# A point-cloud attention kernel: gathers put first in GpSimd's iteration, second-layer maxima subtracted by VectorE, and an inverse root by Newton steps

## The chip, the cores and the metric

The kernel runs on one core of a Trainium2 chip. The metric is the device time of one execution in microseconds (us), the median of several runs. The engines are named as in the profile: PE (TensorE matmuls) and PEld (its weight loads), DVE (VectorE), ACT (ScalarE), POOL (GpSimd) and SP (SyncE, which here only issues DMAs).

## The reference

The reference is a chain of six blocks on `x` of shape (2, 64, 1024). Each reads a layer norm of `x` and adds its result to `x`: a quantised cross attention, a Mamba block, an expert layer, the point-cloud network (`L1_xattn`), a block-masked linear layer and a gated feed-forward layer. The change lies in the point-cloud network. There are two batches of N = 1024 points with 64 features each. Four orderings of the points (two Morton curves and two Hilbert curves) give each point four lists of k = 10 neighbours. Cut to what matters:

```python
def _get_graph_features(feats, inds_list, perm, W_lin, b_lin, k=K):
    for inds in inds_list:                     # four orderings
        neigh = gather(feats, inds)            # B, N, k, C
        gf = concatenate([broadcast(center), neigh - center], axis=-1)
    x = stack(per_method)[..., perm].reshape(B * N, k, total)
    qh = x.astype(float16).astype(float32).reshape(B * N, k, nheads, 64)
    scores = einsum('bihd,bjhd->bhij', qh, qh) / sqrt(64)
    attn = softmax(scores, axis=-1)
    out = einsum('bhij,bjhd->bihd', attn, qh)
    return (out @ W_lin.T + b_lin).reshape(B, N, k, 128)

g1 = _get_graph_features(f0, inds_list, perm1, W_lin1, b_lin1)
h1 = lrelu(instance_norm(einsum('oc,bnkc->bonk', W_conv1, g1)))
feats1 = h1.max(axis=-1)                       # the same again for layer 2, with
...                                            # 128 channels, and a last product
```

The instance norm takes mean and variance over all points and neighbours of a batch, so a batch's first layer has to be finished before its second begins.

## The kernel before

`mamba` (to about 503 us in the trace) holds the first three blocks, `point_cloud` (503 to about 1080 us) the network above, `masked_linear_and_ffn` the rest. The order of every engine's instructions is the order in which the Python code issues them: a manual schedule, with an in-order queue for each engine, and semaphores where one engine needs what another wrote.

`point_cloud` runs four phases: layer 1 for batch 0 and batch 1 (phases 0 and 1), then layer 2 for the same (2 and 3). A phase is 22 sets of 48 points (the last has 16), so there are 88 items, and `iteration(i)` is a software pipeline over them. In one iteration:

- `edges(i + 2)`: POOL subtracts centres from neighbours (`x`, L964); `mended` corrects the first points of a phase on DVE (L974, L976).
- `apart(i + 1)`: the halves of `x` are copied into block form `xz`, the upper half first (layer 2: DVE, L985; layer 1: ACT, L987), the lower half by ACT (L987).
- `turn(i - 2)`: DVE transposes the attention (`at`, L1018). `collect(i - 4)`: DVE takes statistics (L1083) and maxima over neighbours (L1085) of the finished output in PSUM; where a phase ends, `finish` follows.
- `exponentials(i - 1)`: PE adds minus the row maxima to the scores in PSUM, as a product of a negative identity with the broadcast maxima (L1005); ACT takes the exponential (L1007).
- `scores(i)`: PE writes the mask and the products of the edges with themselves into PSUM (L993, L996). `normalize(i - 1)`: DVE sums and inverts (L1012, L1013), POOL multiplies (L1014). `maxima(i)`: DVE (L1000).
- `attend(i - 3)` (PE L1059, L1062, ACT copy L1064), `weighted(i - 1)` (PE: L1032 in layer 1; L1043 with ACT copies L1045 in layer 2), `turn_u` (DVE L1049, layer 1), `back(i - 3)` (PE L1072).

Work that belongs to the next phase is not in this loop's body but in `plan`, a list of (time, closure) pairs that `neighbours` writes. Times are counted in iterations:

```python
def iteration(i):
    todo(i - 0.5)        # everything in plan with a time up to i - 0.5
    edge(i + 2)
    ...
    todo(i)              # everything up to i
```

`neighbours(ph, perm, start)` plans, for a phase that starts at iteration `start`: the features' transposition and the rows' way through DRAM (`begin`, `begin1`, with eight loads of `cen` on SP's queue, L870, at `start - 14.5`), the centre terms (L888 to L904), and the window of neighbours. For this window each of 8 chunks of 128 points takes four indirect DMAs, issued by POOL (`gather`, L925), then a copy on ACT (`rows`, L932), two transposes on PE (`turn`, L937) and a copy out of PSUM on ACT (`put`, L942). Gather m of chunk c has the time `start - lead + (4c + m) * 2 // 3`, so one or two gathers fall to an iteration.

`finish` turns a phase's statistics into mean and inverse deviation, normalises and applies the leaky ReLU. It returns closures that `plan` spreads over the iterations that follow. `rstd` joins the statistics on DVE (L144), takes a square root on ACT (L146) and the reciprocal on DVE (L148). In layer 1 ACT also brings the two halves of `hm` (64 partitions each) together in one tile (L1132 to L1137). The exponential and the square root need different function tables on ACT.

In the last eight iterations with other work (78 to 85) POOL also masks the weights of the next block (L1365), one 128x1024 product in each, behind L1014.

Of the kernel before, what the change touches and what calls it, by code (L numbers as in the profile page):

```python
# [20 lines left out]
P = 128  # L21
D = 1024
KC = D // P
NB = 2
S = 64
EPS = 1e-5
# [10 lines left out]
NP = 1024  # L37
K = 10
NM = 4
TP = 3  # L40
QP = 4 * TP
SG = 48
NBK = SG // TP
# [49 lines left out]
class Kernel:  # L93
# [47 lines left out]
    def rstd(self, pool, st, p=P):  # L141
        nc = self.nc
        mv = self.t(pool, [P, 2], tag="ln_mv")
        nc.vector.bn_aggr(mv[:p], st)  # L144
        sd = self.t(pool, [P, 1], tag="ln_sd")
        nc.scalar.activation(sd[:p], mv[:p, 1:2], AF.Sqrt, bias=self.eps[:p], scale=1.0)  # L146
        r = self.t(pool, [P, 1], tag="ln_r")
        nc.vector.reciprocal(r[:p], sd[:p])  # L148
        return mv[:, 0:1], r

    def layernorm(self, pool, tag="h", update=None):

# [686 lines left out]
    def neighbours(self, ph, perm, start):  # L839
# [4 lines left out]
        nc, ps, layer, b = self.nc, self.g_ps, ph["layer"], ph["b"]  # L844
        o = 64 * layer
        plan = []
# [73 lines left out]
        def gather(c, m):  # L920
            def work():
                if m == 0:
                    ph[c] = self.t(self.g_feat, [P, NM, 64], tag="sl", bufs=3)
                k = self.place[:, b, perm[m], c:c + 1]
                nc.gpsimd.indirect_dma_start(out=ph[c][:, m, :], out_offset=None, in_=ph["src"][:, :],  # L925
                                             in_offset=bass.IndirectOffsetOnAxis(ap=k, axis=0))
            return work

        def place(c):
            def rows():  # L930
                pm = ph["pm"] = self.t(self.g_feat, [P, 4, NM, 16], tag="pm", bufs=2)
                nc.scalar.copy(pm, ph[c].rearrange("p m (h f) -> p h m f", h=4))  # L932

            def turn():
                pm, pt = ph["pm"], self.t(ps, [P, 2, P], tag="misc")
                for hp in range(2):
                    nc.tensor.transpose(pt[:, hp, :], pm[:, 2 * hp:2 * hp + 2].rearrange("p h m f -> p (h m f)"), self.ident)  # L937
                ph["placed"] = pt

            def put():  # L940
                win = ph["win"].rearrange("p n a -> p a n")
                nc.scalar.copy(win[:, :, LPAD + P * c:LPAD + P * c + P], ph["placed"])  # L942
                if c == KC - 1:
                    e = LPAD + NP
# [12 lines left out]

# [31 lines left out]
    def scores(self, it):  # L989

        nc, x, xz, nb = self.nc, it["x"], it["xz"], it["nb"]
        sc = it["sc"] = self.t(self.g_pa, [P, NBK, 32], tag="sc")[:, 0:nb]
        nc.tensor.matmul(sc, self.ident16, self.mask16.unsqueeze(1).to_broadcast([P, nb, 32]), start=True, stop=False, skip_group_check=True)  # L993
        for k in range(nb):
            for hp in range(2):
                nc.tensor.matmul(sc[64 * hp:64 * hp + 64, k, :], xz[:, hp, k].rearrange("p a j -> p (a j)"), x[:, hp, k, :], start=False, stop=False, skip_group_check=True)  # L996

    def maxima(self, it):
        mx = it["mx"] = self.t(self.g_a, [P, NBK], BF16, tag="mx")[:, 0:it["nb"]]
        self.nc.vector.tensor_reduce(mx, it["sc"], AX.X, ALU.max)  # L1000

    def exponentials(self, it):

        nc, nb = self.nc, it["nb"]
        nc.tensor.matmul(it["sc"], self.nident16, it["mx"].unsqueeze(2).to_broadcast([P, nb, 32]), start=False, stop=True, skip_group_check=True)  # L1005
        e = it["e"] = self.t(self.g_a, [P, NBK, 32], tag="e")[:, 0:nb]
        nc.scalar.activation(e, it["sc"], AF.Exp, scale=0.125)  # L1007

    def normalize(self, it):
        nc, nb, e = self.nc, it["nb"], it["e"]  # L1010
# [92 lines left out]
    def norm_lrelu(self, dst, src, mean, r):  # L1103
        nc = self.nc
        nc.vector.tensor_scalar(dst, src, mean, r, ALU.subtract, ALU.mult)
        nc.vector.scalar_tensor_tensor(dst, dst, 0.2, dst, ALU.mult, ALU.max)

    def finish(self, ph):

        nc = self.nc  # L1110
        hm, st, ns = ph["hm"], ph["st"], len(ph["sets"])
        if ph["layer"] == 2:
            f = hm.rearrange("p g n -> p (g n)")[:, :NP]

            def measure():
                ph["stats"] = self.rstd(self.g_hm, st)

            return [measure] + self.norm_lrelu(f, ph, slice(0, P))
# [6 lines left out]
        left = NP - 2 * QP * ng  # L1125

        def measure():
# [12 lines left out]

    def norm_lrelu(self, f, ph, r):
        nc = self.nc

        def norm():
            mean, rs = ph["stats"]
            nc.vector.tensor_scalar(f, f, mean[r], rs[r], ALU.subtract, ALU.mult)

        def lrelu():
            nc.vector.scalar_tensor_tensor(f, f, 0.2, f, ALU.mult, ALU.max)
            ph["out"] = f  # L1150

        return [norm, lrelu]

    def point_cloud(self):
        nc, tc, a = self.nc, self.tc, self.a
        with ExitStack() as es:
            pool = lambda n, b, **k: (self.ctx if k.get("space") is PSUM else es).enter_context(tc.tile_pool(name=n, bufs=b, **k))
# [21 lines left out]
            mean, r = self.rstd(self.g_hm, self.xst)  # L1179
# [68 lines left out]
            def iteration(i):  # L1248


                todo(i - 0.5)
                edge(i + 2)
                if at(i + 1):
                    self.mended(at(i + 1))
                    self.apart(at(i + 1), 1)
                if at(i - 2):
                    self.turn(at(i - 2))
                if at(i - 4):
                    it = at(i - 4)
                    ph, end = it["ph"], it["last"]  # L1260
                    self.collect(it)
                    if end:
                        work = self.finish(ph)
                        if i == last + 3:
                            for w in work:
                                w()
                        else:
# [240 lines left out]
```

## Time and profile before

| | |
|---|---|
| Median of 3 runs | 1145.97 us (1141.42 to 1148.03) |
| Profiled execution: its own time | 1150.54 us |
| Profiled execution: span, first to last instruction | 1148.5 us |
| Mean granted TensorE clock | 0.96 |
| PE / DVE / ACT / POOL busy in the span | 89% / 67% / 53% / 44% |
| L1005 (the matmul that the change removes in layer 2) | 88 in all, 84 of 128x512, mean 390 ns |
| Function table loads on ACT between 503 and 1062 us | 6, 1283 ns each |
| Gathers L925 | 128, mean 996 ns on POOL |

A line of the timeline gives start, length, engine, source line, operation, tiles written and read, and in brackets how long the engine had been idle before and what ended that. A windows line gives the stretch and its length, then the busy time and the number of instructions of PE, PEld, DVE, ACT and POOL, the granted clock, the DMA share and GB/s. Shapes are partitions x elements.

### The profile page before, as it was taken

Reading aid. Unit: us, or ns where it says so; the run is one execution under the profiler, and the core shown is the slowest. Engines: PE = TensorE matmul, PEld = TensorE weight load, DVE = VectorE, ACT = ScalarE, POOL = GpSimd, SP = SyncE. Lnnn points to the kernel's source line nnn. Section 1 sums busy time; section 2 is a strip of 40 time slices with the busy share of each in tenths; the row PEclk is TensorE's granted clock in tenths of the full one; section 3 lists DMA queues with packets and bytes.
Section 4 is the critical chain, followed back from the end, with each engine's and each line's share of the span. In section 5 each row is a group of like instructions: output and inputs, shape, how many; then the busy total and the mean of one; then the engine's idle time right before and its main releaser. Section 6 shows DMA issues by size and latency. Waiting matters only on the chain.

```text
span 1148.5 us, 34713 instructions
## 1 busy us (share of the span) xinstructions
PE 1019.3 (89%) x15331; PEld 752.1 (65%) x15331; DVE 769.6 (67%) x1623; ACT 611.3 (53%) x977; POOL 510.7 (44%) x421
## 2 busy tenths in 40 slices
PE   3899999999999998966877788878998899999898
PEld 1798958769688695533544545557777777788443
DVE  6698865777767764444867887897666767676511
ACT  6333326576575731125756576657676676776110
POOL 0010110102425175068968788786756577683000
PEclk9999989999999998987988889899999999999999
DMA  8677839687596874723221003100303200000460
GB/s 334 264 273 286 344 135 397 242 351 291 232 403 238 341 297 144 245 48 62 51 32 23 12 11 67 35 16 11 66 7 115 81 13 11 9 4 3 180 260 18
DMA packets 48018, 170.93 MB, mean 149 GB/s; under 512 B 26438, under 2 KB 27378, under 8 KB 40956
## 3 DMA queue, kind: packets, MB, share of 16 engines
q1 hardware_dynamic: 37980, 151.83, 35.6%
q10 hardware_dynamic: 3744, 12.65, 3.2%
q0 software_dynamic: 6144, 4.24, 2.1%
q8 instruction: 120, 1.97, 0.7%
q14 instruction: 30, 0.25, 0.1%
HBM read 163.48 MB, written 2.72 MB: 145 GB/s over the span
## 4 chain that ended last, share of the span: by engine, by line
PE 63%; DVE 15%; issue 7%; ACT 7%; POOL 5%; DMA 3%; DVEq 0%; SPq 0%; ACTq 0%; POOLq 0%
PE pin L346 13%; PE misc L1043 11%; PE po L483 7%; PE op L1062 6%; PE sc L996 3%; PE pt L1072 3%; DVE cpre L361 3%; PE sc L1389 3%; PE misc L1032 2%; POOL sl L925 2%; PE misc L1389 2%; POOL x L964 2%; PE op L1059 2%; DVE df L775 2%; ACT xz L987 2%
## 5 line engine op out<-in xcount | busy, mean ns | idle before, releaser
L346 PE MATMUL pin<-hT,w 128*128 128x128 f32 x2320 | 264.8, 276 | 2.0 <-issue 1.7
L346 PEld LDWEIGHTS pin<-hT,w 128*128 128x128 f32 x2320 | 262.7, 193 | 5.6 <-issue 4.9
L964 POOL TENSOR_TENSOR x<-win,cen 128x960 f16<-128x960 f32 x88 | 170.9, 1942 | 5.0 <-ACT win L942 2.8
L1043 PE MATMUL misc<-wz,xz 128*64 128x128 bf16 x4128 | 131.6, 220 | 17.2 <-issue 10.4
L987 ACT COPY xz<-x 64x1024 f16<-64x1024 f16 (+1 forms) x131 | 133.8, 1021 | 18.3 <-DVE x L974 13.3
L925 POOL DMA_INDIRECT sl<-src,place x128 | 127.5, 996 | 31.5 <-issue 20.3
L1014 POOL TENSOR_TENSOR e<-e,z 128x512 f32<-128x512 f32 x88 | 90.6, 1030 | 112.6 <-DVE z L1013 86.2
L1043 PEld LDWEIGHTS <-xz 128*64 128x64 f16 x4128 | 118.9, 110 | 31.5 <-issue 31.2
L1045 ACT COPY u<-misc 128x512 f32<-128x512 f32 x172 | 98.0, 588 | 52.9 <-PE misc L1043 32.3
L460 POOL TENSOR_TENSOR xc<-y,normw 128x512 f32<-128x512 f32 x8 | 8.3, 1038 | 243.5 <-DVE y L458 200.9
L776 ACT ACTIVATE df<-df,neg 128x1024 f32<-128x1024 f32 x64 | 73.4, 1148 | 76.1 <-DVE df L775 62.5
L483 PE MATMUL po<-ow,xc 128*128 128x512 f32 x240 | 109.4, 609 | 0.0
L1062 PE MATMUL op<-u,at 128*32 128x64 f32 (+1 forms) x2752 | 93.1, 257 | 17.6 <-issue 17.5
L361 DVE SCALAR_TENSOR_TENSOR cpre<-craw,convw,cpre 128x126 f32<-128x126 f32 (+2 forms) x240 | 80.6, 357 | 24.3 <-ACT cpre L355 18.7
L759 POOL DMA_INDIRECT place<-cst,rank x64 | 67.0, 1046 | 51.8 <-DVE rank L781 23.7
L1062 PEld LDWEIGHTS op<-u,at 128*32 128x32 f32 x2752 | 65.1, 113 | 33.3 <-issue 26.0
L1083 DVE BATCH_NORM_STATS2 st<-pt 128x6 f32<-128x240 f32 (+1 forms) x84 | 43.4, 517 | 64.7 <-PE pt L1072 57.5
L775 DVE SCALAR_TENSOR_TENSOR df<-hi_r,hl,lo_r 128x1024 f32<-128x1024 f32 x64 | 80.8, 1291 | 3.3 <-DMA lo_r<-rows 1.6
L483 PEld LDWEIGHTS po<-ow,xc 128*128 128x128 f32 x240 | 45.8, 196 | 53.0 <-issue 52.3
L1032 PE MATMUL misc<-x,heads 128*32 128x512 f16 (+1 forms) x1056 | 77.7, 410 | 2.9 <-issue 2.3
L1012 DVE TENSOR_REDUCE z<-e 128x16 f32<-128x512 f32 x88 | 58.5, 665 | 32.3 <-ACT e L1007 28.6
L996 PEld LDWEIGHTS <-xz 128*64 128x64 f16 x2752 | 53.5, 116 | 39.9 <-issue 39.0
(354 smaller groups left out, 1577.6 us busy)
## 6 DMA issues: line engine op xcount, KB each, us to landing
w<-in_in_proj_w SPq DMA_DIRECT2D x36, 2048.0 KB
ow<-in_out_proj_w SPq DMA_DIRECT2D x16, 2048.0 KB
w<-in_L_ffn_w SPq DMA_DIRECT2D x3, 4096.0 KB
ow<-in_ctx SPq DMA_DIRECT2D x4, 1024.0 KB
w<-in_ctx SPq DMA_DIRECT2D x4, 1024.0 KB
hi_r<-rows ACTq DMA_DIRECT2D x8, 512.0 KB
lo_r<-rows ACTq DMA_DIRECT2D x8, 512.0 KB
df<-in_L_attn_mask ACTq DMA_DIRECT2D x8, 512.0 KB
```

The lines of the kernel that those rows point to most:

```text
L346: nc.tensor.matmul(pt[:, c, :], w[:, c, kc, :], hT[:, kc, :], start=(kc == 0), stop=(kc == KC - 1))
L361: nc.vector.scalar_tensor_tensor(pv[:, :, s:], rv[:, :, :S - s], convw[:, cc + c, 3 - s:4 - s], pv[:, :, s:], ALU.mult, ALU.add)
L483: nc.tensor.matmul(st["pq"][n], st["xc"][:, 4 * q + c, :], ow[:, c, 512 * n:512 * n + 512], start=(q == 0 and c == 0), stop=(q == 1 and c ...
L775: V.scalar_tensor_tensor(df, hi_r, hl[:, 0, cc:cc + 1], lo_r, ALU.subtract, ALU.add)
L925: nc.gpsimd.indirect_dma_start(out=ph[c][:, m, :], out_offset=None, in_=ph["src"][:, :], in_offset=bass.IndirectOffsetOnAxis(ap=k, axis=0))
L964: nc.gpsimd.tensor_tensor(xv, over, mid, ALU.subtract)
L987: nc.scalar.copy(dst, src)
L1014: nc.gpsimd.tensor_tensor(e, e, z.unsqueeze(2).to_broadcast([P, nb, 32]), ALU.mult)
L1032: nc.tensor.matmul(pu[32 * h:32 * h + 32], wz[:, j, h // 2, h % 2, 32 * ob:32 * ob + 32], it["x"][:, h // 2, 0:nb, :], start=(j == 0), sto ...
L1043: nc.tensor.matmul(pu[64 * hp:64 * hp + 64, k, :], xz[:, hp, k0 + k].rearrange("p a j -> p (a j)"), wz[j][:, hp, :], start=(j == 0), stop= ...
L1045: nc.scalar.copy(u[:, k0:k0 + kb], pu)
L1062: nc.tensor.matmul(op[32 * r:32 * r + 32, q, :], it["at"][:, 4 * q + r, :], it["u"][:, 4 * q + r, :], start=False, stop=True, skip_group_c ...
```

## The change

It has three parts. In `neighbours` the lead falls by one for phases 1 to 3, and a gather from time 0 on is planned half an iteration earlier than before relative to its time, so that it runs in `todo(i - 0.5)` ahead of `edges`; the copies and transposes behind it get steps to match. In layer 2 the matmul L1005 is left out: DVE subtracts the maxima, reading the scores in PSUM and writing `e` in SBUF, right after it took the maxima, and ACT's exponential works on `e` in place. And the inverse root at the end of phases 0, 1 and 2 (not 3) is computed on DVE from an integer first guess and three Newton steps; in layer 1 the normalisation is done by the ACT operations that bring the two halves together, all four of them now in one iteration.

```diff
+    def rstd_v(self, pool, st, p):
+        nc, ts = self.nc, self.nc.vector.tensor_scalar
+        mv, y, t = (self.t(pool, [P, n], tag=tag)[:p] for n, tag in ((2, "nw_mv"), (1, "nw_y"), (1, "nw_t")))
+        yi, ti = (self.t(pool, [P, 1], I32, tag=tag)[:p] for tag in ("nw_yi", "nw_ti"))
+        def guess():
+            nc.vector.bn_aggr(mv, st)
+            ts(t, mv[:, 1:2], EPS, None, ALU.add)
+            nc.vector.tensor_scalar(ti, t.bitcast(I32), 1, None, ALU.logical_shift_right)
+            ts(yi, ti, -1.0, float(0x5F3759DF), ALU.mult, ALU.add)
+            nc.vector.tensor_copy(y, yi.bitcast(F32))
+        def newton():
+            u = self.t(pool, [P, 1], tag="nw_u")[:p]
+            for _ in range(3):
+                nc.vector.scalar_tensor_tensor(u, y, t, y, ALU.mult, ALU.mult)
+                ts(u, u, -0.5, 1.5, ALU.mult, ALU.add)
+                nc.vector.tensor_tensor(y, y, u, ALU.mult)
+        return mv[:, 0:1], y, guess, newton
...
-        lead, steps = (7, (1, 1, 1.5)) if start == 0 else (9, (1, 2, 2.5))
+        lead = 8 if start else 7
         for c in range(KC):
             for m in range(NM):
-                plan.append((start - lead + (NM * c + m) * 2 // 3, gather(c, m)))
-            for k, w in zip(steps if start or c > 1 else (1, 1, 1) if c == 0 else (2, 2, 2.5), place(c)):
+                t = start - lead + (NM * c + m) * 2 // 3
+                plan.append((t - 0.5 * (t >= 0), gather(c, m)))
+            for k, w in zip((0.5, 1, 1.5) if start or c > 1 else (1, 1, 1) if c == 0 else (2, 2, 2.5), place(c)):
                 plan.append((start - lead + (NM * c + NM - 1) * 2 // 3 + k, w))
...
     def maxima(self, it):
+        nc.vector.tensor_reduce(mx, sc, AX.X, ALU.max)
+        e = it["e"] = self.t(self.g_a, [P, NBK, 32], tag="e")[:, 0:nb]
+        if it["layer"] == 2:
+            nc.vector.tensor_tensor(e, sc, mx.unsqueeze(2).to_broadcast([P, nb, 32]), ALU.subtract)

     def exponentials(self, it):
-        nc.tensor.matmul(it["sc"], self.nident16, it["mx"].unsqueeze(2).to_broadcast([P, nb, 32]), start=False, stop=True, skip_group_check=True)
-        e = it["e"] = self.t(self.g_a, [P, NBK, 32], tag="e")[:, 0:nb]
-        nc.scalar.activation(e, it["sc"], AF.Exp, scale=0.125)
+        if it["layer"] == 1:
+            nc.tensor.matmul(it["sc"], self.nident16, it["mx"].unsqueeze(2).to_broadcast([P, nb, 32]), start=False, stop=True, skip_group_check=True)
+        nc.scalar.activation(e, it["sc"] if it["layer"] == 1 else e, AF.Exp, scale=0.125)
...
     def finish(self, ph):   # layer 1; layer 2, phase 2: guess, newton, normalise on DVE, lrelu
         def measure():
             nc.vector.tensor_copy(sa[:, 0:ns, :], st[lo, 0:ns, :])
             nc.vector.tensor_copy(sa[:, ns:, :], st[hi, :, :])
-            ph["stats"] = self.rstd(self.g_hm, sa, 64)
-            nc.scalar.copy(fv[:, 0:ng, 0, :], hm[lo, 0:ng, :])
-            nc.scalar.copy(fv[:, ng, 0, :], hm[lo, ng, :])
+            guess()
+        def steps():
+            newton()
+            nc.vector.tensor_scalar(off, mean, r, -1.0, ALU.mult, ALU.mult)
+        def even():
+            for v, n in ((fv[:, 0:ng, 0, :], ng), (fv[:, ng, 0, :], None)):
+                nc.scalar.activation(v, hm[lo, 0:n, :] if n else hm[lo, ng, :], AF.Identity, bias=off, scale=r)
         def odd():
-            nc.scalar.copy(fv[:, 0:ng, 1, :], hm[hi, 0:ng, :])
-            nc.scalar.copy(fv[:, ng, 1, 0:left - QP], hm[hi, ng, 0:left - QP])
-        return [measure, odd] + self.norm_lrelu(f[:, 0:NP], ph, lo)
+            nc.scalar.activation(fv[:, 0:ng, 1, :], hm[hi, 0:ng, :], AF.Identity, bias=off, scale=r)
+            nc.scalar.activation(fv[:, ng, 1, 0:left - QP], hm[hi, ng, 0:left - QP], AF.Identity, bias=off, scale=r)
+        def both():
+            even()
+            odd()
+        return [measure, steps, both, lambda: self.lrelu(f[:, 0:NP], ph)]
```

More of the change, by code (lines that the diff above doesn't have):

```diff
@@ L995, in scores @@
             for hp in range(2):
-                nc.tensor.matmul(sc[64 * hp:64 * hp + 64, k, :], xz[:, hp, k].rearrange("p a j -> p (a j)"), x[:, hp, k, :], start=False, stop=False, skip_group_check=True)
+                nc.tensor.matmul(sc[64 * hp:64 * hp + 64, k, :], xz[:, hp, k].rearrange("p a j -> p (a j)"), x[:, hp, k, :], start=False, stop=(it["layer"] == 2), skip_group_check=True)
     def maxima(self, it):
-        mx = it["mx"] = self.t(self.g_a, [P, NBK], BF16, tag="mx")[:, 0:it["nb"]]
-        self.nc.vector.tensor_reduce(mx, it["sc"], AX.X, ALU.max)
+        nc, nb, sc = self.nc, it["nb"], it["sc"]
+        mx = it["mx"] = self.t(self.g_a, [P, NBK], BF16, tag="mx")[:, 0:nb]
+        nc.vector.tensor_reduce(mx, sc, AX.X, ALU.max)
+        e = it["e"] = self.t(self.g_a, [P, NBK, 32], tag="e")[:, 0:nb]
+        if it["layer"] == 2:
+            nc.vector.tensor_tensor(e, sc, mx.unsqueeze(2).to_broadcast([P, nb, 32]), ALU.subtract)
     def exponentials(self, it):
-        nc, nb = self.nc, it["nb"]
-        nc.tensor.matmul(it["sc"], self.nident16, it["mx"].unsqueeze(2).to_broadcast([P, nb, 32]), start=False, stop=True, skip_group_check=True)
-        e = it["e"] = self.t(self.g_a, [P, NBK, 32], tag="e")[:, 0:nb]
-        nc.scalar.activation(e, it["sc"], AF.Exp, scale=0.125)
+        nc, nb, e = self.nc, it["nb"], it["e"]
+        if it["layer"] == 1:
+            nc.tensor.matmul(it["sc"], self.nident16, it["mx"].unsqueeze(2).to_broadcast([P, nb, 32]), start=False, stop=True, skip_group_check=True)
+        nc.scalar.activation(e, it["sc"] if it["layer"] == 1 else e, AF.Exp, scale=0.125)
     def normalize(self, it):
@@ L1113, in finish @@
             f = hm.rearrange("p g n -> p (g n)")[:, :NP]
-            def measure():
-                ph["stats"] = self.rstd(self.g_hm, st)
-            return [measure] + self.norm_lrelu(f, ph, slice(0, P))
+            if ph["b"] == NB - 1:
+                mean, r = self.rstd(self.g_hm, st)
+                nc.vector.tensor_scalar(f, f, mean, r, ALU.subtract, ALU.mult)
+                return self.lrelu(f, ph)
+            mean, r, guess, newton = self.rstd_v(self.g_hm, st, P)
+            return [guess, newton, lambda: nc.vector.tensor_scalar(f, f, mean, r, ALU.subtract, ALU.mult), lambda: self.lrelu(f, ph)]
         lo, hi = slice(0, 64), slice(64, P)
@@ L1125, in finish @@
         left = NP - 2 * QP * ng
+        mean, r, guess, newton = self.rstd_v(self.g_hm, sa, 64)
+        off = self.t(self.g_hm, [64, 1], tag="nw_off")
         def measure():
@@ L1129, in measure, with lrelu @@
             nc.vector.tensor_copy(sa[:, ns:, :], st[hi, :, :])
-            ph["stats"] = self.rstd(self.g_hm, sa, 64)
-            nc.scalar.copy(fv[:, 0:ng, 0, :], hm[lo, 0:ng, :])
-            nc.scalar.copy(fv[:, ng, 0, :], hm[lo, ng, :])
-        def odd():
-            nc.scalar.copy(fv[:, 0:ng, 1, :], hm[hi, 0:ng, :])
-            nc.scalar.copy(fv[:, ng, 1, 0:left - QP], hm[hi, ng, 0:left - QP])
-        return [measure, odd] + self.norm_lrelu(f[:, 0:NP], ph, lo)
[L1141 to L1152, printed above, removed]
+            guess()
[5 more added lines that the diff above has]
+                nc.scalar.activation(v, hm[lo, 0:n, :] if n else hm[lo, ng, :], AF.Identity, bias=off, scale=r)
+        def odd():
+            nc.scalar.activation(fv[:, 0:ng, 1, :], hm[hi, 0:ng, :], AF.Identity, bias=off, scale=r)
[4 more added lines that the diff above has]
+        return [measure, steps, both, lambda: self.lrelu(f[:, 0:NP], ph)]
+    def lrelu(self, f, ph):
+        self.nc.vector.scalar_tensor_tensor(f, f, 0.2, f, ALU.mult, ALU.max)
+        ph["out"] = f
     def point_cloud(self):
@@ L1263, in iteration @@
                         work = self.finish(ph)
[L1264 to L1267, printed above, removed]
+                        if work:
                             plan.extend((i + k, w) for k, w in enumerate(work))
```

## The prediction

> **What bounds the kernel now.** I read the page first (busy shares, the chain that ended last), then the timeline of single iterations of the point-cloud part, then windows and groups for the prices.
>
> ```profile
> span 1148.5 us, 34713 instructions
> PE 1019.3 (89%) x15331; PEld 752.1 (65%) x15331; DVE 769.6 (67%) x1623; ACT 611.3 (53%) x977; POOL 510.7 (44%) x421
> PE 63%; DVE 15%; issue 7%; ACT 7%; POOL 5%; DMA 3%; DVEq 0%; SPq 0%; ACTq 0%; POOLq 0%
> ```
>
> The change touches only the 88 iterations between 515 and 1058 us. The windows view, cut at the maxima (L1000) that open each phase, gives their lengths and PE's busy time in the first column:
>
> ```profile
> 531.46:650.84 119.38, 96.67 (x2027) 59.20 (x2030) 90.96 (x181) 76.28 (x112) 97.66 (x79) 0.90 0.16 28
> 650.84:770.32 119.48, 98.66 (x2142) 62.73 (x2142) 100.69 (x205) 77.84 (x118) 95.67 (x77) 0.92 0.17 31
> 770.32:920.29 149.97, 134.42 (x3644) 110.89 (x3647) 103.85 (x184) 104.34 (x182) 98.99 (x77) 0.99 0.21 55
> 920.29:1058.15 137.86, 131.37 (x3708) 110.06 (x3701) 92.25 (x159) 98.65 (x167) 95.56 (x69) 0.99 0.04 8
> ```
>
> The first layer (two phases of 119 us, 5.4 us an iteration) has no engine over 84%: DVE, POOL and PE hand work to one another. In the second layer PE is busy 90 and 95%. One of its iterations, in the timeline:
>
> ```profile
> 1015.50 0.38 PE L1005 MATMUL sc<-mx,nident 128*128 128x512 bf16 x1
> 1015.70 0.67 DVE L1083 BATCH_NORM_STATS2 st<-pt 128x6 f32<-128x480 f32 x1 [1.45 <-PE pt L1072]
> 1015.72 0.38 PE L993 MATMUL sc<-mask,ident 128*128 128x512 bf16 x1
> 1017.55 0.25 DVE L1013 RECIPROCAL z<-z 128x16 f32<-128x16 f32 x1
> 1017.72 0.63 DVE L1000 TENSOR_REDUCE mx<-sc 128x16 bf16<-128x512 f32 x1
> 1017.95 1.05 POOL L1014 TENSOR_TENSOR e<-e,z 128x512 f32<-128x512 f32 x1 [0.72 <-DVE z L1013]
> 1018.38 0.90 DVE L985 COPY xz<-x 64x1024 f16<-64x1024 f16 x1
> ```
>
> Maxima to maxima this iteration takes 5.75 us (1011.97 to 1017.72), PE has no idle time in it, and DVE waits 1.45 us for PE at L1083. The matmul that the change removes, L1005, sits on PE's line: L993 follows 0.22 us later. Iterations with one gather take 6.1 us, with two 7.4.
>
> Two places in which everything waits. First, a statistics step at a phase's end: ACT loads the square-root table, DVE stands 3.65 us before the reciprocal, ACT loads the exponential's table, PE loses 2.94 us:
>
> ```profile
> 791.24 1.28 ACT L146 ACT_TABLE_LOAD   x1
> 792.86 0.15 DVE L148 RECIPROCAL ln_r<-ln_sd 64x1 f32<-64x1 f32 x1 [3.65 <-ACT ln_sd L146]
> 793.74 1.28 ACT L1007 ACT_TABLE_LOAD   x1
> 797.57 0.64 PE L1043 MATMUL misc<-wz,xz 128*64 128x128 bf16 x16 [2.94 <-ACT u L1045]
> ```
>
> Second, in phase 0 a gather meets eight loads of `cen` on SP's queue and lands 6.8 us after its issue; ACT, in order, stands at L932 with all else behind it:
>
> ```profile
> 569.98 4.97 SPq L870 DMA_DIRECT2D cen<-rows  x8
> 570.80 0.98 POOL L925 DMA_INDIRECT sl<-src,place  x1 [0.16 <-issue]
> 577.67 0.41 ACT L932 COPY pm<-sl 128x256 f32<-128x256 f32 x1 [4.51 <-DMA sl<-src,place]
> ```
>
> **Part 1, the gathers.** For phases 1 to 3 the lead falls by one (9 to 8) and the half step puts a gather at the head of an iteration, not at the end of the one before: on POOL that is the same place, so nothing moves there. In phase 0 the lead stays 7, so each gather from time 0 on runs one iteration earlier, and its L932 too. The gather above (its time 8) moves to the slot of 566.70, 3.3 us ahead of the `cen` loads. The two iterations that it spoilt took 9.14 and 7.79 us; their neighbours 4.4 to 5.7, and the second holds 1.65 us of L888 of its own, so 6.2 us come back. Four gathers in a row (602.03 to 606.77, L1062 stuttering in 2.9 us of issue gaps) become two and two: minus 1.5, at worst 0. Against it, one or two gathers (1.0 and 0.30 us gap each) now stand before L964 while phase 0 starts, where POOL is busy 3.66 of 3.82 us: plus 1.5, bounds 0 and 2.7. What is late next is chunk 6: its first two gathers now meet the `cen` loads, but are wanted two iterations later. Sum minus 6, bounds minus 9 and plus 2.
>
> **Part 2, three statistics steps on DVE.** The iteration with the step takes 8.87, 10.22 and 9.83 us; over the five iterations around each, where PE also runs slow after the gap (32 of L996 in 1.04 us at 676.55, against 0.68), I find 6, 4.2 and 1.3 us more than five ordinary ones: 11.5. Both table loads, the root and DVE's wait go. Added are 4 small operations, and 9 or 10 in the next iteration; such 1-element rows take 0.13 to 0.17 us and start 0.18 apart, so 2.5 us a step; the normalisation (0.77 to 1.28 us) leaves DVE for ACT in layer 1, where it replaces copies of the same size (0.60). In layer 2 DVE's 1.45 us of idle time and more in an ordinary iteration hide it; in layer 1, where DVE is busy 4.0 of 4.4 us, nothing does: 2.5 less the normalisation, plus 1.5 once. Sum minus 10, bounds minus 13 and plus 3.
>
> Six Newton operations read two tensors from SBUF. Rows for such: L974 and L976, 18 elements, take 0.16 us beside no POOL tensor work and 2.6 us where L964 got ahead (525.30, 761.09). I take none, since they follow L1014 while POOL is in gathers; the upper bound takes three hits of 1.5 a step. The Trainium skill, SBUF — State Buffer, "Who interferes with whom", says that a DVE instruction with two SBUF inputs is blocked by a GpSimd instruction that reads SBUF, for that whole instruction; by that rule every one of the six is exposed, and the sum of this part would be plus 3. The trace's two long rows agree.
>
> The Trainium skill, ScalarE: Activation LUTs, "What ACT_TABLE_LOAD costs", puts a switch at 1.28 us and a drain of 1.38 more; by it six switches would be 16 us of ACT. Here L1007 starts 1.29 us after the load at 793.74, so no drain shows.
>
> **Part 3, the maxima on DVE.** PE loses L1005, 0.22 us, in 44 iterations. DVE gains a 128x512 difference of PSUM and a broadcast bf16; the nearest row is L897 (PSUM minus bf16, 108x512): 0.65 to 0.69 us, and 0.675 at 844.30 with L1014 beside it, so no lock. ACT's exponential reads SBUF, same length (0.60), and stops waiting for PE (0.2 us). DVE's 0.66 lies in its idle time. It also pushes L985: now L985 starts inside L1014 and takes 0.90; alone it takes 0.42 (845.01, just behind L1014, where the gather beside it stretches from 1.00 to 1.12). After the change it would start 0.04 us after L1014 ends. With gathers next on POOL that is a gain of 0.48 for DVE. So in the 34 iterations with gathers: 34 x 0.21 = minus 7.1, bounds minus 7.5 and 0.
>
> In eight later iterations POOL follows L1014 at once with L1365 (2.1 us; in time before: 0.05 us ahead of L1014's end). There L985 comes too late and waits, as at 853.45, where L964 was ahead and it took 2.09. DVE's round is then: reciprocal's end to L1014's end 1.20, L1365 2.0, rest of L985 0.28, L1018 0.73, L1083 0.58, L1085 0.56, L1012 0.71, L1013 0.25: 6.31 us, against 5.77. Eight times 0.54: plus 4.3. If L985 slips in first: minus 1.8. I take plus 4.3, less 0.4 for two iterations without L1365.
>
> **Sum.** -6 - 10 - 7.1 + 3.9 = minus 19.2. The profiled execution took 1150.54 us, 4.6 over the median of 1145.97: 1131.3 for it, and 1126.8 for the median, which I give as 1127.
>
> **Rivals.** (a) The gather's wait only moves to chunk 6 behind the same `cen` loads: part 1 gives nothing, 1133. For: SP's loads keep their place. Against: two iterations of room. (b) Newton steps meet the lock three times a step: part 2 gives plus 3, 1140. For: L976's 2.6 us. Against: their place behind L1014. (c) L1005's removal doesn't do what it says: PE's stops around gathers (0.29 us in one-gather iterations, 1.4 in two-gather ones, from when the gather is issued) set the end of these iterations, and the 0.21 is lost in them: 1134. Against: PE's own work fills the rest. (d) Slower: DVE becomes the bound. If L985 comes over 1.1 us behind L1014's end, L964 has the lock in the 17 one-gather iterations too; the round is then 1.20 + 1.15 + 1.97 + 0.28 + 0.73 + 0.58 + 0.56 + 0.71 + 0.25 = 7.43, against 6.1: plus 23, and their 3.6 of part 3 lost: 1154. It decides at a difference taking 1.7 us, not 0.66; L897 speaks against it.
>
> **Numbers.** Forecast 0.53, (a) 0.15, (b) 0.12, (c) 0.12, (d) 0.08. A measurement of this kernel tells about 0.5% from no change, so the line lies at 1140: forecast, (a) and (c) are faster, 0.80; (b) is same, 0.12; (d) slower, 0.08. Lower end: the low bounds of parts 1 and 2, 44 x 0.22 and minus 1.8, together minus 33: 1113. Upper end 1143: beyond (b), short of (d).
>
> **What would show it.** No table load between 540 and 1058 us; no wait of over 2 us at L932 in phase 0; the difference at 0.65 to 0.70; L985 at 0.42 where gathers run, at 2 us beside L1365; second-layer iterations of 5.9 and 7.1 us with one and two gathers. It is wrong if DVE shows no idle time in one-gather iterations, or small rows of Newton of over 1 us.

## The result, and the profile after

The changed kernel takes 1129.24 us (median of 4 runs, 1126.91 to 1133.36) against 1146.88 for the kernel before (4 runs, 1141.42 to 1148.03) beside it. The ratio is 0.987, with a 95% interval of 0.9829 to 0.991: 15 us faster, 10 to 20 (the two medians alone differ by 17.6). The forecast was 1127, and its range 1113 to 1143 holds the result. The sum behind it is another matter: of its three parts one, the Newton steps, gave nothing, and the other two together gave more than was worked out for them.

The profiled execution of the changed kernel took 1129.23 us. Its page begins so (span; busy time by engine; the chain that ended last):

```profile
span 1127.2 us, 34732 instructions
PE 1005.5 (89%) x15287; PEld 748.0 (66%) x15287; DVE 811.6 (72%) x1703; ACT 604.7 (54%) x968; POOL 510.0 (45%) x421
PE 58%; DVE 23%; ACT 7%; issue 6%; DMA 4%; POOL 1%; SPq 1%; DVEq 0%; ACTq 0%
```

DVE gained 42 us of work and 8 points of the chain; PE lost 14 us of work and 5 points. The windows view, cut at the maxima (now L1025) that open the four phases, as before:

```profile
531.50:640.73 109.23, 90.68 (x2032) 57.23 (x2032) 89.62 (x181) 75.62 (x111) 96.64 (x78) 0.97 0.17 31
640.73:762.90 122.17, 98.93 (x2136) 62.96 (x2136) 106.11 (x217) 76.29 (x115) 95.49 (x77) 0.93 0.16 31
762.90:909.17 146.27, 134.96 (x3638) 112.89 (x3637) 118.48 (x218) 102.53 (x179) 98.08 (x77) 0.95 0.21 56
909.17:1039.16 129.99, 126.23 (x3715) 108.10 (x3714) 117.01 (x195) 96.41 (x165) 96.09 (x69) 1.00 0.04 9
```

Against before: phase 0 is 10.2 us shorter, phase 1 is 2.7 us *longer*, phase 2 is 3.7 and phase 3 7.9 shorter; 2.3 more come after it. The first maxima stand where they stood (531.46 and 531.50). Phase 1 holds none of part 3 and, by the prediction's own working, none of part 1, so that the Newton step won nothing there. How much it lost this pair of traces can't tell: the traces of the runs below without part 2 on this level have 118.0 to 121.5 us for phase 1.

**Phase 0.** The wait of 4.51 us at the copy of a gathered slab is gone. In the timeline after, the longest such wait in the phase is this one (the copy is now L955, the gather L948; in the timelines here and below, rows between those shown are left out):

```profile
553.03 0.95 POOL L948 DMA_INDIRECT sl<-src,place  x1 [0.30 <-issue]
...
556.15 0.41 ACT L955 COPY pm<-sl 128x256 f32<-128x256 f32 x1 [1.10 <-DMA sl<-src,place]
```

Items 9 and 10 take 5.26 and 5.62 us, where they took 9.14 and 7.79: minus 6.0, as worked out. Items 13 and 14, behind the four gathers in a row, went from 6.06 and 8.71 to 5.06 and 5.03: minus 4.7, where 1.5 was expected. The clock column may hold the rest: 0.90 for this phase before, 0.97 after. Before, two stretches of 6.83 us run at 0.50, one beginning at each of these two places, where PE had stood, and neither is there after (windows views, two before, then one after):

```profile
577.86:584.69 6.83, 6.56 (x97) 3.67 (x98) 2.31 (x5) 4.49 (x7) 3.39 (x4) 0.50 0.10 15
605.17:612.00 6.83, 4.70 (x37) 3.25 (x37) 2.76 (x6) 1.20 (x3) 6.14 (x6) 0.50 0.17 29
```

```profile
602.00:612.00 10.00, 8.69 (x196) 5.47 (x194) 8.42 (x18) 7.72 (x12) 9.14 (x8) 1.00 0.16 27
```

The prediction priced the stop beside the four gathers, not the slow stretch that came with it. The gathers at the head of items 0 to 8 cost 0.9 us there (42.20 against 41.33), where 1.5 was expected.

**A statistics step.** No table load is left between 503 and 1041 us. But one of Newton's operations waits (timeline, POOL and DVE in item 26, then the leaky ReLU L1182 in item 28):

```profile
663.79 0.99 POOL L948 DMA_INDIRECT sl<-src,place  x1
664.11 2.69 DVE L168 SCALAR_TENSOR_TENSOR nw_u<-nw_y,nw_t 64x1 f32<-64x1 f32 x1
664.80 1.98 POOL L988 TENSOR_TENSOR x<-win,cen 128x960 f16<-128x960 f32 x1
666.83 0.15 DVE L169 TENSOR_SCALAR nw_u<-nw_u 64x1 f32<-64x1 f32 x1
667.01 0.15 DVE L170 TENSOR_TENSOR nw_y<-nw_y,nw_u 64x1 f32<-64x1 f32 x1
667.20 0.21 DVE L168 SCALAR_TENSOR_TENSOR nw_u<-nw_y,nw_t 64x1 f32<-64x1 f32 x1
...
678.50 1.98 POOL L988 TENSOR_TENSOR x<-win,cen 128x960 f16<-128x960 f32 x1
678.63 2.94 DVE L1182 SCALAR_TENSOR_TENSOR f<-f 64x1024 f32<-64x1024 f32 x1
```

The row at 664.11 ends 0.02 us after L988 does; the same operation takes 0.21 us at 667.20, with POOL idle. At 791.16 and 934.90 one L168 takes 2.56 and 2.54 us in the same way: one hit in each of the three steps, some 2.4 us each.

**A second-layer iteration with two gathers** (item 77, 6.66 us; before 7.33). PE and DVE in the timeline after:

```profile
974.03 2.87 PE L1071 MATMUL misc<-wz,xz 128*64 128x128 bf16 x96
975.12 0.69 DVE L1028 TENSOR_TENSOR e<-sc,mx 128x512 f32<-128x512 f32 x1
975.85 0.50 DVE L1009 COPY xz<-x 64x1024 f16<-64x1024 f16 x1
975.89 0.99 POOL L948 DMA_INDIRECT sl<-src,place  x1
978.67 0.54 PE L1020 MATMUL sc<-x,xz 128*64 128x32 f16 x22 [0.46 <-issue]
```

The difference takes 0.69 us and the copy 0.50, as worked out. The whole of L1071 runs through, and PE stops once, for 0.46 us, in L1020. In the same item before, L1043 (the same line) was caught in mid-run, in these two places and for 0.13 us in a third:

```profile
996.16 0.34 PE L1043 MATMUL misc<-wz,xz 128*64 128x128 bf16 x5 [0.40 <-issue]
...
996.90 0.43 PE L1043 MATMUL misc<-wz,xz 128*64 128x128 bf16 x8 [0.40 <-issue]
```

So items 75 to 77 (two, one, two gathers) went from 20.99 to 18.70 us: 0.21 each for the removed matmul, and most of the rest from PE's stops, which come to 0.84 us in the three items and came to 2.00 before.

**The eight mask iterations.** The copy L1009 meets the mask product L1393 and takes 2.05 us, as forecast:

```profile
999.96 0.69 DVE L1028 TENSOR_TENSOR e<-sc,mx 128x512 f32<-128x512 f32 x1
1000.53 1.92 POOL L1393 TENSOR_TENSOR w_attn<-w_attn,on 128x1024 f32<-128x1024 f32 x1
1000.68 2.05 DVE L1009 COPY xz<-x 64x1024 f16<-64x1024 f16 x1
```

Maxima to maxima these take 6.06 us, against 5.77. Yet item 86 then takes 3.93, and the time from the last maxima to the end is 2.3 us shorter. The experiments settle what that means.

### The profile page after: what moved, and what is told of

Same layout as the page of the kernel before. It is cut to its first block, busy times and chain, and to the rows that moved or that the text cites. A ratio compares the mean times of both kernels' runs of the same rounds, so it can differ in the third digit from the quotient of the medians.

```text
span 1127.2 us, 34732 instructions
## 1 busy us (share of the span) xinstructions
PE 1005.5 (89%) x15287; PEld 748.0 (66%) x15287; DVE 811.6 (72%) x1703; ACT 604.7 (54%) x968; POOL 510.0 (45%) x421
## 4 chain that ended last, share of the span: by engine, by line
PE 58%; DVE 23%; ACT 7%; issue 6%; DMA 4%; POOL 1%; SPq 1%; DVEq 0%; ACTq 0%
PE pin L369 11%; PE misc L1071 9%; PE po L506 7%; PE op L1090 6%; PE sc L1020 4%; PE misc L1060 3%; PE pt L1100 3%; DVE cpre L384 3%; PE sc L1417 3%; DMA df<-in_L_attn_mask 2%; PE misc L1417 2%; DVE df L798 2%; ACT df L799 2%; PE op L1087 2%; PE sc L1017 1%
## 5 line engine op out<-in xcount | busy, mean ns | idle before, releaser
L988 POOL TENSOR_TENSOR x<-win,cen 128x960 f16<-128x960 f32 x88 | 171.6, 1951 | 4.0 <-DMA bias<-in_L_ffn_b 2.6
L948 POOL DMA_INDIRECT sl<-src,place x128 | 127.6, 997 | 31.5 <-issue 21.1
L1071 PE MATMUL misc<-wz,xz 128*64 128x128 bf16 x4128 | 130.8, 221 | 9.0 <-issue 7.6
L1071 PEld LDWEIGHTS <-xz 128*64 128x64 f16 x4128 | 119.9, 111 | 21.0 <-issue 20.4
L799 ACT ACTIVATE df<-df,neg 128x1024 f32<-128x1024 f32 x64 | 73.4, 1147 | 75.6 <-DVE df L798 66.3
L1090 PE MATMUL op<-u,at 128*32 128x64 f32 (+1 forms) x2752 | 95.8, 258 | 16.4 <-issue 15.4
L1090 PEld LDWEIGHTS op<-u,at 128*32 128x32 f32 x2752 | 65.6, 112 | 33.4 <-issue 26.3
L1060 PE MATMUL misc<-x,heads 128*32 128x512 f16 (+1 forms) x1056 | 75.4, 396 | 2.2 <-issue 1.8
L1020 PEld LDWEIGHTS <-xz 128*64 128x64 f16 x2752 | 53.0, 115 | 36.5 <-issue 35.6
L1040 DVE TENSOR_REDUCE z<-e 128x16 f32<-128x512 f32 x88 | 58.2, 662 | 22.1 <-ACT e L1035 19.2
L1100 PE MATMUL pt<-cst,oT 128*128 128x128 f32 x258 | 48.5, 295 | 20.6 <-ACT oT L1092 10.2
```

The source lines that it names most:

```text
L988: nc.gpsimd.tensor_tensor(xv, over, mid, ALU.subtract)
L1060: nc.tensor.matmul(pu[32 * h:32 * h + 32], wz[:, j, h // 2, h % 2, 32 * ob:32 * ob + 32], it["x"][:, h // 2, 0:nb, :], start=(j == 0), sto ...
L1071: nc.tensor.matmul(pu[64 * hp:64 * hp + 64, k, :], xz[:, hp, k0 + k].rearrange("p a j -> p (a j)"), wz[j][:, hp, :], start=(j == 0), stop= ...
L1090: nc.tensor.matmul(op[32 * r:32 * r + 32, q, :], it["at"][:, 4 * q + r, :], it["u"][:, 4 * q + r, :], start=False, stop=True, skip_group_c ...
```

## The experiments

The runs came in four series, each on one chip with its own runs of the kernel before beside it. The kernel before took 1105.51 and 1104.25 us in the first two and 1148.46 and 1147.84 in the last two; the first and the last ran on the same chip. The mean granted clock is about the same in all (medians of 0.963 and 0.957 to 0.958), so it is another level of the same program, and neither the clock nor the chip tells the two apart: at 0.965 to 0.967 the kernel before takes 1102 to 1106 us on the one and 1137 to 1142 on the other. Each comparison below stays in its series unless it says otherwise. The prediction and its result stand on the long level.

### The parts by themselves, short level

Each is the kernel before with the hunks of one part of the diff above and nothing else. **Part 1 alone**:

```diff
-        lead, steps = (7, (1, 1, 1.5)) if start == 0 else (9, (1, 2, 2.5))
+        lead = 8 if start else 7
...
+                plan.append((t - 0.5 * (t >= 0), gather(c, m)))
```

> The kernel before with part 1 alone. Theory on record: minus 6 us, median near 1140. Theory from the two traces: the whole lead that the changed kernel has won by the 24th iteration, 10.0 us, is part 1, and nothing of it is lost later: minus 10, median near 1136, and the fourth to the tenth iteration show no wait of over 2 us at L932's copy. Rival (a) of the prediction: the wait moves to chunk 6 and part 1 gives nothing, 1146.

Measured: 1105.48 against 1105.51, ratio 0.9996 (0.9983 to 1.0008): nothing, within 2 us. **Part 2 alone**:

```diff
-            ph["stats"] = self.rstd(self.g_hm, sa, 64)
+            guess()        # and steps() an iteration later, both() after it
```

> The kernel before with part 2 alone. Theory on record: minus 10 us, 1136. Rival (b): three hits of the lock a step, plus 3, 1149. Theory from the trace of after: one hit a step of 2.3 to 2.5 us (row L168: 2.69, 2.56, 2.54 against 0.21), one longer lrelu in layer 1 (2.94 against 1.17), so that of the 11.5 us won 9 are given back: minus 2, 1144.

Measured: 1107.73, ratio 1.0013 (0.9995 to 1.0031): plus 1.4 us, from minus 0.6 to plus 3.4. One L168 in each step takes 2.68 to 2.74 us. The forecast of minus 10 is out; so is minus 2. Plus 3, the prediction's rival (b), lies inside the interval. **Part 3 alone**:

```diff
-        nc.tensor.matmul(it["sc"], self.nident16, it["mx"]...)    # layer 2
+            nc.vector.tensor_tensor(e, sc, mx..., ALU.subtract)   # layer 2
```

> The kernel before with part 3 alone. Theory on record: minus 7.1 plus 3.9, so minus 3, 1143. Theory from the trace of after: iterations with two gathers 0.67 shorter and with one 0.52 shorter, where PE stops less around the gathers, eight mask iterations 0.28 longer, and a drain after the last iteration 2.3 and one iteration 1.85 shorter: minus 9, 1137. Rival (c): the removal is lost in PE's stops: 0 to plus 4, 1146 to 1150.

Measured: 1098.95, ratio 0.992 (0.9893 to 0.9946): minus 8.8, from 6.0 to 11.8. That falls on the second expectation, the one from the trace of after, and rules out minus 3 on this level.

### Newton's operations with one tensor

The changed kernel, its two-tensor operations written with a column as the scalar operand; nothing else differs:

```diff
-                nc.vector.scalar_tensor_tensor(u, y, t, y, ALU.mult, ALU.mult)
+                ts(u, y, y, t, ALU.mult, ALU.mult)
...
-                nc.vector.tensor_tensor(y, y, u, ALU.mult)
+                ts(y, y, u, None, ALU.mult)
```

> The changed kernel with the six two-tensor operations of a Newton step written as operations of one tensor with one-column scalars (u = y*y*t and y = y*u), same count and order. If the lock asks for two tensor inputs, no Newton row is over 0.3 us and the three hits of 2.3 to 2.5 us go: minus 5 to minus 7 against the changed kernel, 1122 to 1124. If a column given as a scalar counts as a second input, one row a step stays at 2.5 us and the time stays at 1129. If the hits lie beside PE's work and cost nothing, the rows go and the time stays at 1128 to 1129.

Measured: 1091.03 us, ratio to before 0.9866 (0.9841 to 0.9892). The changed kernel itself was run on this level in the next series.

> The changed kernel as it is, beside the kernel before and the two versions sent with it. On a chip where the kernel before takes 1146: 1129. On one where it takes 1105, as in the four runs above: if the parts add up (gathers 0, Newton plus 2, maxima minus 7), 1100 to 1101; if the lead of part 1 is real there too, 1095.

Measured: 1098.19 against 1104.25, ratio 0.994 (0.9919 to 0.9961), minus 6.6 us. The three parts by themselves sum to -0.4 + 1.4 - 8.8 = -7.8, so they add up within their intervals.

### The copy ahead of the difference

```diff
+                if at(i - 1) and self.late(at(i - 1)):   # the last ten items
+                    self.difference(at(i - 1))            # behind apart(at(i + 1), 1)
```

> The changed kernel with the subtraction of the last ten iterations moved behind the copy L1009 on VectorE, so that the copy starts inside L1042 and not inside L1393. Theory: the copy takes 0.90 us in place of 2.05, VectorE's round falls below PE's, the eight mask iterations go from 6.06 to 5.55 us (5.77 less the 0.22 of the removed matmul): minus 4 against the changed kernel. Rival: the exponential, 1 us later, now sets the round, and they stay over 5.9: 0 to minus 1.

The copy takes 0.90 us and the mask iterations 5.55, both as expected:

```profile
966.91 0.90 DVE L1009 COPY xz<-x 64x1024 f16<-64x1024 f16 x1
```

The time is 1099.13, ratio 0.9943 (0.9923 to 0.9962): no gain over the 0.994 of the changed kernel. The windows view says why. One mask iteration of the kernel before, of the changed kernel and of this one, PE's busy time and matmuls in the first column:

```profile
1017.72:1023.49 5.77, 5.77 (x178) 4.92 (x174) 4.22 (x8) 4.46 (x7) 5.02 (x3) 1.00 0.01 3
```

```profile
999.30:1005.35 6.05, 6.05 (x195) 5.31 (x191) 5.94 (x9) 4.80 (x9) 5.03 (x3) 1.00 0.01 4
```

```profile
966.25:971.81 5.56, 5.56 (x174) 4.82 (x169) 4.83 (x10) 4.39 (x7) 5.03 (x3) 1.00 0.03 7
```

PE has no idle time in any of them. In the changed kernel it does 195 matmuls between two maxima, more than one iteration's worth: it had work in hand, and the 6.06 us is DVE's own round, not PE's. In this trace of the changed kernel the work in hand runs out in the last of these rounds. In items 84 and 85 PE stops for 0.33 and 0.29 us, until DVE has taken the maxima over neighbours:

```profile
1022.78 0.65 PE L1100 MATMUL pt<-cst,oT 128*128 128x128 f32 x4 [0.33 <-DVE hm L1113]
1028.70 0.66 PE L1100 MATMUL pt<-cst,oT 128*128 128x128 f32 x4 [0.29 <-DVE hm L1113]
```

From the maxima of item 78 to the last statistics step (the L144 behind item 87) the kernels without part 3 take 64.28 us (before, part 1 alone and part 2 alone, both levels, to 0.01), those with it 61.87 to 61.99, this one 61.98. That is 2.3 less for ten matmuls of 0.22 us, wherever the copy stands. By that count, many more mask iterations would have let DVE's round set the pace; no run has more.

**Both edits together:**

> The changed kernel with both edits: the one-tensor form of the Newton steps and the copy ahead of the subtraction. If the three hits of the lock cost 2.3 us each and the copy 0.5 us in eight iterations, and nothing else takes their place, minus 9 to minus 11 against the changed kernel. If PE hides the hits, minus 4.

Measured: 1090.82, ratio 0.9882 (0.9862 to 0.9902), minus 13.0 us. Against the run with the copy alone, in the same series, that is 0.9882 / 0.9943: minus 6.8 us for the one-tensor form, some 3 either way. Three hits of 2.3 us would be 7.0. In the two traces the items of the hits (26, 48 and 70) are 2.2, 1.4 and 1.2 us shorter, 4.8 in all, so that a good part of the hits lay on the path, not shown to be all.

### The gather and the loads of `cen`

```diff
-            for r in range(8):
+            for r in [*range(8)] * (2 if start else 1):      # in e9 and e10
                 nc.sync.dma_start(ph["cen"][16 * r:16 * r + 16, :, :NP], rv[r // 4])
```

> The kernel before with part 1 alone, a second time, beside the two that follow. On a chip where the kernel before takes 1146 and the gather beside the loads of cen lands after 6.8 us: minus 10, 1136. On one where it takes 1105 (in the run with part 2 alone the same gather landed after 3.2 us): 0, within 1.5.

> The kernel before with each of the 24 loads of cen of the later phases issued twice, part 1 not in it. Theory: the loads hold the gather that is issued 0.8 us behind them, so it lands later by about the time of eight more loads, and the wait at L932 in the tenth iteration of phase 0 grows from 1 to 2 us to 4 or more: plus 3 to plus 6 against the kernel before. Rival: the loads have nothing to do with the wait, which is the gather's own time on that chip: 0.

> The same doubled loads, with part 1. Theory: the gather goes out one iteration ahead of the loads and does not meet them; the next one to meet them is wanted two iterations later: 0 to plus 1 against the kernel before, 3 to 5 less than with the loads doubled and part 1 left out. Rival (a): the wait moves to the next chunk, and both take the same.

This series fell on the long level. Part 1 alone: 1141.55 against 1148.46, ratio 0.9952 (0.9922 to 0.9981), minus 5.5 us, from 2.2 to 9.0; its phase 0 takes 109.40 us in the trace, which is of the fastest of its runs (1134.79). Times on this level go with the mean granted clock: the kernel before ranges in this series from 1139.48 us at 0.966 to 1155.53 at 0.953. Whether the clock makes the time, or both follow from PE's stops, none of the runs separates. The loads doubled without part 1: ratio 1.006 (1.0027 to 1.0093), plus 6.9; with it: 1.0014 (0.9977 to 1.005). That looks like the expectation, but the traces deny its mechanism. With the loads doubled the wait is 4.47 us, not longer than the 4.51 of before:

```profile
567.98 9.89 SPq L870 DMA_DIRECT2D cen<-rows  x14
568.79 0.99 POOL L925 DMA_INDIRECT sl<-src,place  x1 [0.16 <-issue]
...
575.62 0.41 ACT L932 COPY pm<-sl 128x256 f32<-128x256 f32 x1 [4.47 <-DMA sl<-src,place]
```

The loads behind the gather do not hold it; phase 0 takes 119.01 us, as before. The doubling adds loads behind the gather only, so those ahead of it stay untested. The added time lies in phase 2 (159.6 us, and 161.1 with part 1, against 150.0 before and 151.2 with part 1 alone), much of it in item 54 (12.07 us, against 8.13 before and 5.63 with part 1 alone), where PE stands 4 us and the profile names nothing that it waits for:

```profile
845.26 0.92 PE L1043 MATMUL misc<-wz,xz 128*64 128x128 bf16 x26 [4.01 <-issue]
```

With part 1 a later slab does meet the doubled loads (3.35 us of wait), and phase 0 is still 7.1 us shorter.

### Part 2 and the one-tensor form, long level

The same two kernels as above.

> The kernel before with part 2 alone, a second time. On a chip where the kernel before takes 1105: plus 1.5, within 2, as in the first run. On one where it takes 1146: theory on record minus 10; theory of one hit of the lock a step, minus 2 to plus 3, since layer 1's second phase is 2.7 us longer in the changed kernel there with no other part touching it.

> The changed kernel with the one-tensor form of the Newton steps, a second time. On a chip where the kernel before takes 1105: minus 13 to minus 15 against it, as in the first run. On one where it takes 1146, where the changed kernel gained 15 to 18: if the three hits lie on the path there too, minus 20 to minus 25; if PE's stops around gathers hide them, minus 17.

Part 2 alone: 1147.89 against 1147.84, ratio 1.0013 (0.9987 to 1.0039), plus 1.5 us, from minus 1.5 to plus 4.5. The changed kernel with the one-tensor form: 1120.17, ratio 0.9771 (0.9729 to 0.9814), minus 26.3 us (21.4 to 31.1), where the changed kernel gained 14.9 on this level, in the result's series. Its six runs have a granted clock of 0.964 to 0.969; the two runs of the kernel before that reached 0.965 in this series took 1136.62 and 1139.13 us, and against these the gain is 16 to 19. Its rows, in the same place:

```profile
662.22 0.99 POOL L948 DMA_INDIRECT sl<-src,place  x1
662.53 0.22 DVE L168 TENSOR_SCALAR nw_u<-nw_y,nw_t 64x1 f32<-64x1 f32 x1
663.21 0.26 DVE L168 TENSOR_SCALAR nw_u<-nw_y,nw_t 64x1 f32<-64x1 f32 x1
663.22 1.97 POOL L988 TENSOR_TENSOR x<-win,cen 128x960 f16<-128x960 f32 x1
663.93 0.27 DVE L168 TENSOR_SCALAR nw_u<-nw_y,nw_t 64x1 f32<-64x1 f32 x1
...
673.45 1.20 DVE L1182 SCALAR_TENSOR_TENSOR f<-f 64x1024 f32<-64x1024 f32 x1
```

All nine operations pass, six of them beside L988, none over 0.27 us, and L1182, now ahead of L988, takes 1.20 us in place of 2.94. Phase 1 takes 114.55 us against 122.17. Of these 7.6 us, 2.2 are item 26, with the hit, and 3.1 item 28, with the leaky ReLU that the hit pushed into L988's time. In item 38 a third two-tensor operation (L927) takes 0.38 us in place of 1.78 and the item 4.17 in place of 6.94. That item takes 4.17 us in the kernel before too, so this can't be put down to the one-tensor form. It is the fastest version of the study on this level.

The traces can be compared more closely. The twelve iterations in which the three steps and what they delay lie (items 25 to 28, 47 to 50, 69 to 72) take, in all:

| | short level | long level |
|---|---|---|
| without part 2 | 72.5, 73.0 us | 78.7, 80.1, 81.3, 81.6 us |
| with part 2 | 78.3, 78.4, 78.7 | 82.0, 82.3 |
| with the one-tensor form | 73.6, 73.6 | 74.3 |

So the hits and what they push cost 5 us in these iterations on the one level and 8 on the other. Without hits the Newton steps win 4 to 7 us on the long level, and nothing on the short one.

The part 2 run also shows what the level is. The same slab of the same kernel, with the same eight loads of `cen` beside it (their row is shown for the first only), long level first and then short, on the same chip:

```profile
569.38 4.85 SPq L893 DMA_DIRECT2D cen<-rows  x8
570.26 0.99 POOL L948 DMA_INDIRECT sl<-src,place  x1 [0.16 <-issue]
...
577.01 0.40 ACT L955 COPY pm<-sl 128x256 f32<-128x256 f32 x1 [4.46 <-DMA sl<-src,place]
```

```profile
563.69 0.99 POOL L948 DMA_INDIRECT sl<-src,place  x1 [0.16 <-issue]
...
566.90 0.40 ACT L955 COPY pm<-sl 128x256 f32<-128x256 f32 x1 [1.33 <-DMA sl<-src,place]
```

From the gather's issue to the copy it is 6.75 us on the one and 3.21 on the other. That fits a part 1 that gained on one level alone: on the other the wait is 1.3 us and not 4.5.

## Why the prediction was right, point by point

The sum was -6 - 10 - 3.2 = -19.2, and -14.9 was measured. On its level part 1 measured -5.5 and part 2 +1.5, in other series, which leaves -10.9 for part 3 by difference. None of the runs measured part 3 alone there, and the three intervals together leave it about 6 us either way; if part 1 is worth the 10 us of its traces, some 6.5 are left for part 3. Parts 1 and 3 together are surer: some 16 us, where 9.2 were forecast. That the total came near was luck: part 2 missed by 11 us, and the other two made up some 7 of it.

**Part 1, minus 6: right in size.** The two spoilt iterations gave the 6.0 of the sum. The four gathers in a row were under-sized (4.7 against 1.5). Phase 0 takes 118.9 to 119.4 us in the traces without part 1 on this level and 109.2 to 109.4 in those with it (the doubled loads left out), 10 less, and the timed runs show 5.5 (2.2 to 9.0). The trace of part 1 alone gives nothing of the 10 back, so the difference between the two is open. Rival (a), the wait at chunk 6, did not come. The cause that the prediction named, loads of `cen` on SP's queue, is only half supported: the slab lands late beside them on the long level, but more of them behind it do not make it later, and on the short level, with the same loads, the copy waits 1.3 us and part 1 wins nothing.

**Part 2, minus 10: wrong.** The step that failed is the sentence "I take none, since they follow L1014 while POOL is in gathers". They do follow it, and a gather is on POOL when the hit begins; but L988 stands behind that gather. The prediction's own two long rows (525.30 and 761.09) say as much: a gather had begun 0.36 us before each, and the row of L964, whose end they waited for, begins 0.6 us later. In layer 1 the forecast said 6 less and 1.5 more; phase 1 became 2.7 longer. Rival (b) had the mechanism and nearly the price (plus 3), with three hits a step; there is one, since after it the rest of the step runs with POOL's product done. What the hit moves adds to its price (the leaky ReLU). The hits explain the whole miss on the prediction's level, as far as two series tell: +1.5 with them, and 11.4 less without them (5 to 18), which is the minus 10 of the sum. On the short level they do not: +1.4 less 6.8 is -5.4, and the table of the twelve iterations has no gain at all without hits. There the 11.5 us put down for the square root's path were too many as well; why is open. The rule of the Trainium skill that the prediction quoted and set aside (SBUF — State Buffer, "Who interferes with whom": a DVE instruction with two SBUF inputs is blocked by a GpSimd instruction that reads SBUF) held: 2.54 to 2.69 us at L168 and none in the one-tensor form. The same section says that an instruction with at most one SBUF input outside the two-port modes does not contend; the rows of 0.26 and 0.27 us beside L988 agree.

**Part 3, minus 3.2: the mechanism right, its two terms off.** The difference (0.66 forecast, 0.69), L1009 where gathers run (0.42 forecast; 0.42 to 0.50 in 23 of 34 items, 0.55 to 2.67 in ten) and L1009 beside L1393 (2 us forecast, 2.05) came as worked out in the main. The term of plus 4.3 had the round's length nearly right (6.31 forecast, 6.06 measured) and its meaning wrong: it took DVE's round for the iteration, and PE, with work in hand nearly to the end, set it. The last ten items took 2.3 us less, where about 3.9 more had been forecast. Gather iterations of 5.9 and 7.1 us were forecast; 5.59 and 6.45 to 6.66 came in items 75 to 77, where PE stops less, and 7.10 to 7.36 in the two-gather items 57, 59 and 61. The stops of 0.29 and 1.4 us on which rival (c) went are those of the weight loads' rows (PEld); PE's own in items 76 and 77 before are 0.14 and 0.92. And the low end of the range counted the mask iterations' 1.8 us twice, since the 44 matmuls hold them.

Rivals (c) and (d) are out: part 3 alone is 8.8 us faster on the short level, and by difference faster on the long one too, and in the one-gather item 76 DVE is busy 4.6 of 5.6 us. In item 74 it is busy 5.0 of 5.1, which by the prediction's own mark would speak for (d); but that round is shorter than the 6.11 us of before, not longer.

## What to carry to other kernels

A small operation with two SBUF tensors can cost what the GpSimd product queued next to it costs: give one operand as a scalar column, which here won 6.8 us on one level and some 11 on the other (the second from two series, 5 to 18). Before a longer round of one engine is priced, count what the engine that sets the end does in that round: 195 matmuls in 6.05 us against 178 in 5.77 was no loss, for as long as PE had work in hand. A sum that comes out right has to be tested part by part; here an error of 11 us in one part was mostly made up by 7 in the others.

## What the runs showed of the hardware that was not expected

- A gather on POOL covered a two-tensor DVE operation only at its beginning. With L988 queued next, operations that began 0.26 us or less after the gather's start passed (L170 at 790.98, 0.15 us), and those that began 0.36 to 0.48 us after it waited for the end of L988 (L1000 at 631.03, 2.66 us; L168 at 791.16, 2.56), though L988's own row begins 0.5 to 0.7 us later. Between, at 0.27 to 0.32 us, both outcomes are seen (L170 at 934.70 took 0.16 and L927 at 715.90 in the one-tensor version its 0.65; L168 at 664.11 waited, and in the runs with part 2 alone it waited at 0.27 to 0.29). The corrections at a phase's start meet this in every kernel of the study: the kernel before has four such rows, 2.62 to 2.67 us each, all begun 0.36 to 0.37 us after a gather. Where the gather's row is 1.80 us long, begun while L1182 still ran on DVE, the copy L1009 passed 0.94 us after the gather's start (805.79, 0.42).
- The same program has two levels, 1105 and 1147 us, with nearly the same mean granted clock. With part 2 alone the two traces differ by 36.6 us: 6.4 have arisen by 478 us, ahead of the point-cloud part, and the four phases, where gathers run, hold 30. The first layer's phases take 118.85 and 126.06 us on the long level (at a clock of 0.90 and 0.85), 109.73 and 115.86 on the short one (0.90 and 0.91), and the last iterations without gathers take the same to 0.01 us. On the long level PE stops for 0.8 us in the two-gather item 77 of that kernel (6.38 us busy of 7.21); on the short level the item takes 5.77 with no stop. What sets the level is open.
